# A graph attention layer and a mean-aggregation layer on one core: the neighbour lists cut into finer steps, the projected rows stored from another queue, and the second layer's products put in another order

## The chip, the core and the metric

The kernel runs on one core of a Trainium2 chip. A core has five engines that run side by side, each with its own instruction stream, executed in order: TensorE (PE in the profile, with PEld for the loading of its weights) for matrix products, VectorE (DVE), ScalarE (ACT), GpSimd (POOL) and SyncE (SP), which here only issues transfers. ACT and POOL can issue transfers too; each issuing engine has its own DMA queue, and 16 DMA engines serve all of them. On-chip data lies in SBUF, with 128 partitions; products are summed in PSUM. What is compared is the device time of one launch in microseconds (us).

## What is computed

Two layers over a graph of 4096 nodes with 512 features. `adj` is a 4096 x 4096 matrix of int32 zeros and ones, in which about one entry in a thousand is one, so a row has some four neighbours.

```python
# layer 0: attention with 8 heads of 64, then residual and layer norm
Wh = einsum('nf,hfo->hno', x, W)
f1 = einsum('hno,ho->hn', Wh, a[:, :64])
f2 = einsum('hno,ho->hn', Wh, a[:, 64:])
e = leaky_relu(f1[:, :, None] + f2[:, None, :], 0.2)
e = where(adj > 0, e, NEG_INF)
x = layernorm(x + einsum('hnm,hmo->hno', softmax(e), Wh))   # heads side by side

# layer 1: mean of the neighbours, two linear maps, a combining map, residual, layer norm
agg = mask @ x / maximum(deg, 1.0)
self_f, nb_f = x @ W_self + b_self, agg @ W_nb + b_nb
x = layernorm(x + relu(concat([self_f, nb_f]) @ W_comb + b_comb))
```

## The kernel before

The nodes are cut into 32 blocks of 128. Nothing of the 4096 x 4096 products is formed: the kernel turns each row of `adj` into a short list of neighbours, and then fetches the neighbours' rows with indirect transfers. All instructions stand in an order written out by hand; generators (`yield`) let a long piece of work be laid in portions between the blocks, one portion at each `next`; `some(lists)` takes one portion of each list in hand.

**First stage, the lists.** A loop over `b` does one block of `adj` per turn. SP loads `adj` in halves of 1 MB into four buffers, two blocks ahead (`load_adj`, L384), and blocks of `x` eight ahead (`load_x`, L317). ACT turns each half into bf16 masks (`mask_adj`, L393), which frees its buffer. PE folds the mask into keys in PSUM (`fold_adj`, L407), and DVE takes the largest (`max_keys`, L423). After every fourth block a `decode` (L430) turns the keys of four blocks into lists: bit operations (to L448), three passes of maxima per block (L454 to L456), counts and the first three neighbours (L459 to L469), ranks and placing matrices for the further ones (`lt` and `st`, L484 and L485), two shared slots (L494 to L518) and the owners of these slots (`own`, L520). It has six portions, and it is taken together with the one before it. `late_lists` (L529) then prepares for the first `NE` = 7 blocks which neighbours lie near the end of the graph. Beside it the nodes are projected: `transposed` (L325), two halves of products (`node_half`, L334), `node_rest` (L343), and `store` (L902), which writes the row of Wh and of f2 to the table `t0` in DRAM from ACT's queue, one turn later. A row has two buffers. Block 0 is projected ahead of the loop, so that block b + 1 falls in turn b, and from turn `AHEAD` = 10 block b + 2. The weights of layer 1 are multiplied together on the way: `m1` = W_self times the upper half of W_comb in this stage, `m2` = W_nb times the lower half between the stages (`fold_weights`, L267).

**The turn.** Behind the last `store` GpSimd gathers the rows of block 0 (L961) and so on: five indirect transfers per block, one per list slot, into `GA` = 5 buffers. Meanwhile the last lists and `m2` are worked on.

**Second stage, the attention.** The loop over `i` is a pipeline over blocks, in which weights (L626), exponentials, denominators (L636), weighted rows (L668), shared slots (`a_shared`, L680), layer norm, a transposition, and `z` = x times m2 (`a_z`, L716) follow each other. `z` goes to the table `t1`, the transposed x to `xt`. The rest of `m2`, the last `decode` and a sum of biases are laid between the turns i = -2 to 11.

**Third stage, the mean.** The first blocks are gathered from `t1` before its last rows are written: for blocks below NE, early gathers fetch what is there (`gather_early`, L604, 5 transfers a block), and one more per block brings the late rows when all of `t1` is written (`gather_late`, L607). For the others 5 full gathers a block go into `GB` = 7 buffers. Per block PE adds the product with m1 (`g_self`, L749, two blocks ahead), the shared slots (`g_shared`, L756) and for the first NE the late ones (`g_late`, L763); DVE sums the other slots (`g_adds`, L734) and forms the moments (`g_moments`, L772); ACT ends the norm (`g_norm`, L782), and SP stores the rows.

Of the kernel before, what the change touches and what calls it, by code (L numbers as in the profile page):

```python
# [56 lines left out]
NE = 7  # L57
# [33 lines left out]
def listed_layers(  # L91
# [33 lines left out]
    AHEAD = 10  # L125
# [141 lines left out]
    def fold_weights(loaded, m, place, tags):  # L267

        wr, wc = loaded

        def turned(c):
            tp = ps.tile([P, FB, P], F32, name="sm", bufs=2)
            for d in range(FB):
                nc.tensor.transpose(tp[:, d, :], wr[:, c, ts(d, P)], ident)
            wT = place(c)
            nc.scalar.copy(wT, tp.rearrange("p c r -> p (c r)"))
            return wT.rearrange("p (c r) -> p c r", c=FB)

        wT = turned(0)
        for c in range(FB):  # L280
            nxt = turned(c + 1) if c + 1 < FB else None
            yield
            tag = tags[c % 2]
            mp = ps.tile([P, HD], F32, name=tag, bufs=1 if tag in ("key", "tp") else 2)
            for d in range(FB):
                nc.tensor.matmul(
                    mp, lhsT=wT[:, d, :], rhs=wc[:, d, :], start=(d == 0), stop=(d == FB - 1)
                )
                if d % 2:
                    yield  # L290
            nc.scalar.copy(m[:, c, :], mp)
            wT = nxt
# [59 lines left out]
    def mean_row(w_sb, xacc, wp):  # L352
# [24 lines left out]
        nc.scalar.dma_start(t0[1:2, 0:H], mf)  # L377
        nc.scalar.dma_start(t0[1:2, H:TW], mr[0:1, 0:HD])
# [51 lines left out]
    def decode(b0, dp, place, slow=False):  # L430
# [4 lines left out]
        for k in range(2):  # L435
# [4 lines left out]
            nc.vector.tensor_sub(kk[:, :, k + 1, :], kk[:, :, k, :], top.bitcast(F32))  # L440
        kf = kk.rearrange("p g a c -> p (g a c)")
        ki = dp.tile([P, G * 3 * NC], I32, name="ki", bufs=1)
        nc.vector.tensor_copy(ki, kf)
        nc.vector.tensor_scalar(ki, ki, SC - 1, None, OP.bitwise_and)
        ke = dp.tile([P, G * 3 * NC], I32, name="ke", bufs=1)
# [7 lines left out]
        for g in range(G):  # L453
# [3 lines left out]
            if slow or g == G - 1:  # L457
                yield
# [11 lines left out]
        yield  # L470
# [4 lines left out]
        dg = dp.tile([P, G], F32, name="dg", bufs=1)  # L475
        nc.vector.tensor_scalar(dg, deg[:, bs], 1.0, None, OP.max)
        nc.vector.reciprocal(L[:, :, KL + 1], dg)

        sts = []
        for b in range(b0, b0 + G):  # L480
# [6 lines left out]
            if slow or b == b0 + G - 1:  # L487
                yield
        for g in range(G):
            if b0 + G < LB - G:  # L490
                nc.gpsimd.tensor_copy(of[:, b0 + g, :], sts[g])
            else:
                nc.scalar.copy(of[:, b0 + g, :], sts[g])
        pe = ps.tile([P, G, KH, EX + H], F32, name="sm", bufs=2)  # L494
        for g in range(G):
            for k in range(KH):
# [3 lines left out]
                )  # L500
        nc.vector.tensor_copy(es[:, bs], pe[:, :, :, 0:EX])
# [25 lines left out]
        )  # L527

# [67 lines left out]
    def gather(table, b, pool, at=None):  # L596
        g = pool.tile([P, KS, TW], F32, name="g")
# [273 lines left out]
    m1s = fold_weights(loaded, m1, lambda c: xs[:, NB - 12 + c, :], ("nm", "nm"))  # L871
    for k in range(3):
        next(m1s)
    bcol = bias_columns(brw)
    biased = fold_bias(loaded, bcol[:, 0:FB])
    for b in range(XL):
        sum_x(b, xacc)


    def node_block(w, xT, between=None):  # L880
# [6 lines left out]
        node_rest(w, row)  # L887
        return row
# [13 lines left out]
    def store(w, row):  # L902
        nc.scalar.dma_start(t0[2 + w * P : 2 + (w + 1) * P, :], row[:, 0:TW])

    row = node_block(0, xT)
    for k in range(3):
        next(m1s)
    xT = transposed(1, wp)
    for h in range(NH):
        mask_adj(0, h)  # L910
    key_bank(0)
    load_x(XL)
    sum_x(XL, xacc)
    w, lists = 1, []
    for b in range(LB):
        for k in range(1 + (b == AHEAD)):
            load_x(w + k + XL)
            sum_x(w + k + XL, xacc)
# [3 lines left out]
        some(lists)  # L922
# [61 lines left out]
    for k in range(3):  # L984
        some(lists)
# [529 lines left out]
```

## Time and profile before

| | us |
|---|---|
| three runs: median (lowest, highest) | 692.93 (691.37, 694.28) |
| the profiled execution, whole | 695.46 |
| its span, which all times below count from | 693.8 |
| PE busy, share of the span | 620.6, 89% |
| DVE busy | 495.9, 71% |
| ACT busy | 439.1, 63% |
| POOL busy | 383.4, 55% |

| stage, by the first and last instructions of its groups in the trace | from, to |
|---|---|
| halves of `adj` masked by ACT (L395) | 30.5 to 242.7 |
| first gather of the attention (L591) to last product of `a_z` (L719) | 238.5 to 493.0 |
| first `g_shared` of the mean (L758) to the end | 494.2 to 693.8 |

Engine rows count the time in which an instruction ran; a transfer that GpSimd issues counts there as busy for the time that its issue takes, and the data land some microseconds later. An engine can be busy for 89% on average and still be the limit in one stage and not in another, so the stages are read one by one.

### The profile page before, as it was taken

Reading aid. Unit: us, or ns where it says so; the run is one execution under the profiler, and the core shown is the slowest. Engines: PE = TensorE matmul, PEld = TensorE weight load, DVE = VectorE, ACT = ScalarE, POOL = GpSimd, SP = SyncE. Lnnn points to the kernel's source line nnn. Section 1 sums busy time; section 2 is a strip of 40 time slices with the busy share of each in tenths; the row PEclk is TensorE's granted clock in tenths of the full one; section 3 lists DMA queues with packets and bytes.
Section 4 is the critical chain, followed back from the end, with each engine's and each line's share of the span. In section 5 each row is a group of like instructions: output and inputs, shape, how many; then the busy total and the mean of one; then the engine's idle time right before and its main releaser. Section 6 shows DMA issues by size and latency. Waiting matters only on the chain.

```text
span 693.8 us, 8911 instructions
## 1 busy us (share of the span) xinstructions
PE 620.6 (89%) x2354; PEld 340.8 (49%) x2354; DVE 495.9 (71%) x1415; ACT 439.1 (63%) x922; POOL 383.4 (55%) x435
## 2 busy tenths in 40 slices
PE   5997989879899688999999999999869999999992
PEld 2565757547576444444545554555323444444430
DVE  6035877898896877999889899988322566565654
ACT  2377877775787634756677777766423566666754
POOL 6532222332211277766566677757776777777760
PEclk9999999999999889999999999999989999999996
DMA  8899999999999977888788999978988899999991
GB/s 269 327 382 320 399 406 407 407 407 385 322 404 375 347 232 230 273 262 255 214 260 277 273 280 281 272 253 263 307 241 266 282 306 317 311 305 304 305 305 72
DMA packets 94040, 209.89 MB, mean 303 GB/s; under 512 B 13649, under 2 KB 13657, under 8 KB 93982
## 3 DMA queue, kind: packets, MB, share of 16 engines
q1 hardware_dynamic: 61968, 111.95, 43.7%
q0 software_dynamic: 26160, 86.40, 42.0%
q10 hardware_dynamic: 5854, 10.90, 4.2%
q8 instruction: 21, 0.34, 0.2%
q14 instruction: 37, 0.30, 0.1%
HBM read 175.52 MB, written 33.69 MB: 302 GB/s over the span
## 4 chain that ended last, share of the span: by engine, by line
PE 50%; DVE 22%; DMA 9%; issue 6%; POOL 4%; ACT 4%; DVEq 0%; ACTq 0%; SPq 0%; POOLq 0%
PE pw L719 11%; PE pw L337 7%; PE nm L751 6%; PE nm L682 6%; PE pw L751 6%; POOL g L591 4%; PE pw L758 3%; PE nm L758 3%; DMA xT<-xt 2%; PE tp L329 2%; DMA g<-t,idx 2%; DVE row L341 2%; DMA t<-row 2%; PE sm L655 1%; DVE kk L428 1%
## 5 line engine op out<-in xcount | busy, mean ns | idle before, releaser
L591 POOL DMA_INDIRECT g<-t,idx x285 | 272.4, 956 | 109.6 <-issue 71.0
L337 PE MATMUL pw<-w_sb,xT 128*128 128x264 f32 x512 | 131.9, 403 | 15.8 <-DVE row L341 15.8
L395 ACT ACTIVATE ab<-at 128x2048 bf16<-128x2048 int32 x64 | 122.0, 1907 | 23.9 <-DMA at<-in_adj_dram 19.4
L719 PE MATMUL pw<-wr,xT 128*128 128x512 f32 x256 | 117.7, 602 | 0.7 <-ACT xT L331 0.7
L337 PEld LDWEIGHTS pw<-w_sb,xT 128*128 128x128 f32 x512 | 94.3, 194 | 44.9 <-DVE row L341 17.6
L323 POOL TENSOR_TENSOR xacc<-xacc,xs 128x512 f32<-128x512 f32 x32 | 41.3, 1291 | 81.3 <-DMA xs<-in_x_dram 80.9
L670 DVE TENSOR_TENSOR g<-g,key 128x1024 f32<-128x1024 f32 x64 | 77.9, 1216 | 1.1
L719 PEld LDWEIGHTS pw<-wr,xT 128*128 128x128 f32 x256 | 46.3, 190 | 47.3 <-issue 46.1
L682 PE MATMUL nm<-g,own 128*128 128x512 f32 x128 | 62.7, 612 | 0.0
L751 PE MATMUL nm<-m,xT 128*128 128x512 f32 x128 | 58.0, 596 | 4.5 <-DMA xT<-xt 4.5
L341 DVE COPY row<-pw 128x264 f32<-128x264 f32 x64 | 26.9, 422 | 47.9 <-PE pw L337 35.3
L751 PE MATMUL pw<-m,xT 128*128 128x512 f32 x128 | 57.8, 594 | 1.5 <-ACT nm L742 1.5
L348 POOL COPY f1s<-lst 128x24 f32<-128x24 f32 x32 | 11.7, 367 | 79.1 <-DVE lst L344 44.7
L331 ACT COPY xT<-tp 128x512 f32<-128x512 f32 x64 | 37.2, 582 | 26.2 <-PE tp L329 19.5
L705 ACT ACTIVATE xs<-y,ln_sum 128x512 f32<-128x512 f32 x32 | 23.1, 722 | 43.2 <-DVE y L698 43.2
L774 DVE SCALAR_TENSOR_TENSOR sm<-y,lst,nm 128x512 f32<-128x512 f32 x16 | 12.1, 755 | 49.8 <-PE nm L768 27.9
L329 PEld LDWEIGHTS tp<-ident,xs 128*128 128x128 f32 x256 | 30.0, 144 | 34.2 <-ACT xs L714 24.9
L329 PE MATMUL tp<-ident,xs 128*128 128x128 f32 x256 | 40.2, 280 | 7.1 <-ACT xs L714 5.8
L751 PEld LDWEIGHTS nm<-m,xT 128*128 128x128 f32 x128 | 24.1, 191 | 37.3 <-issue 32.1
L591 POOL DMA_INDIRECT g<-t,idxe x35 | 33.1, 947 | 15.4 <-issue 8.5
L751 PEld LDWEIGHTS pw<-m,xT 128*128 128x128 f32 x128 | 24.1, 190 | 32.2 <-issue 28.4
L742 ACT COPY nm<-brow 128x512 f32<-128x512 f32 x16 | 9.4, 590 | 44.3 <-DVE sm L774 44.3
(208 smaller groups left out, 1076.8 us busy)
## 6 DMA issues: line engine op xcount, KB each, us to landing
at<-in_adj_dram SPq DMA_DIRECT2D x64, 1024.0 KB, 9.2
t<-row ACTq DMA_DIRECT2D x32, 260.0 KB, 6.0
xt<-xT SPq DMA_DIRECT2D x32, 256.0 KB
t<-row SPq DMA_DIRECT2D x32, 256.0 KB, 3.9
xT<-xt SPq DMA_DIRECT2D x32, 256.0 KB, 7.9
out_dram<-row SPq DMA_DIRECT2D x32, 256.0 KB, 4.1
xs<-in_x_dram SPq DMA_DIRECT2D x31, 256.0 KB, 12.7
g<-t,idx POOLq DMA_INDIRECT x285, 4.6
```

What stands on the lines that cost most here:

```text
L323: nc.gpsimd.tensor_tensor(xacc, xacc, xs[:, b, :], OP.add)
L329: nc.tensor.transpose(tp[:, c, :], xs[:, b, ts(c, P)], ident)
L331: nc.scalar.copy(t, tp)
L337: nc.tensor.matmul(pw, lhsT=xT[:, c, :], rhs=w_sb[:, c, k * HW : (k + 1) * HW], start=(c == 0), stop=(c == FB - 1),)
L341: nc.vector.tensor_copy(row[:, k * HW : (k + 1) * HW], pw)
L395: nc.scalar.activation(ab, loads.pop((b, h)), AF.Relu, accum_out=asum[:, b, h : h + 1])
L591: nc.gpsimd.indirect_dma_start(out=out, out_offset=None, in_=table, in_offset=bass.IndirectOffsetOnAxis(ap=at, axis=0),)
L670: nc.vector.tensor_tensor(gv if to is None else to.rearrange("p (k h d) -> p k h d", k=1, h=H), gv, E[b][:, sl].unsqueeze(3).to_broadcast( ...
L682: nc.tensor.matmul(NM[b], lhsT=OWN[b][:, k, :], rhs=G0[b][:, K0 + k, H:TW], start=False, stop=(k == KH - 1), skip_group_check=True,)
L719: nc.tensor.matmul(pz, lhsT=xT[:, c, :], rhs=m2[:, c, :], start=(c == 0), stop=(c == FB - 1))
L751: nc.tensor.matmul(NM[b], lhsT=xT[:, c, :], rhs=m1[:, c, :], start=False, stop=(c == FB - 1), skip_group_check=True,)
L758: nc.tensor.matmul(NM[b], lhsT=OWN[b][:, k, :], rhs=g[:, K0 + k, 0:HD], start=False, stop=(k == KH - 1), skip_group_check=True,)
```

## The change

Six things are changed together.

1. The first stage starts with the lists: block 0 of `adj` is masked and its keys begun before the loop, block 0 is projected in turn 0 beside its own list, and two turns (14 and 19) project two blocks. `sum_x` runs four blocks behind the loads of x.
2. `m1` is folded in eight half columns, one in turn 0 and in every odd turn, instead of in full at the start; the second half is added by DVE.
3. `decode` has 16 portions, of which four are taken per turn (two before the block, two after), so that one is done when the next begins. Between the counts and the ranks three portions pass, and the copies of the placing matrices come behind the products that read them. `late_lists` starts two turns later, with `NE` = 6.
4. Wh rows are stored from GpSimd's queue right behind the block. The weights of `m2` are loaded by SP's queue.
5. Between the stages the decode of blocks 24 to 27 is finished, twelve of sixteen portions of `m2` are done, and half of the last decode; the rest goes into turns -2 to 6.
6. In the third stage `g_shared` and `g_late` of a block stand ahead of `g_self` of the block after next, and block 6 is gathered in full. A gather buffer is made once and filled slot by slot.

```diff
-NE = 7
+NE = 6
-    AHEAD = 10
+    AHEAD = (14, 19)
...
+    def turned(wr, c, wT):
+        tp = ps.tile([P, FB, P], F32, name="sm", bufs=2)
+        for d in range(FB):
+            nc.tensor.transpose(tp[:, d, :], wr[:, c, ts(d, P)], ident)
+        nc.scalar.copy(wT, tp.rearrange("p c r -> p (c r)"))
+        return wT.rearrange("p (c r) -> p c r", c=FB)
+    def fold_halves(loaded, m, place):
+        wr, wc = loaded
+        wT = turned(wr, 0, place(0))
+        yield
         for c in range(FB):
+            for k in range(2):
+                mp = ps.tile([P, HD], F32, name="nm", bufs=2)
+                for d in range(2 * k, 2 * k + 2):
+                    nc.tensor.matmul(
...
+                if k == 0:
+                    nc.scalar.copy(m[:, c, :], mp)
+                else:
+                    nc.vector.tensor_add(m[:, c, :], m[:, c, :], mp)
+                    if c + 1 < FB:
+                        wT = turned(wr, c + 1, place(c + 1))
+                yield
+    def fold_quarters(loaded, m, place):
+        wr, wc = loaded
+        wT = turned(wr, 0, place(0))
+        for c in range(FB):
+            nxt = turned(wr, c + 1, place(c + 1)) if c + 1 < FB else None
+            mp = ps.tile([P, HD], F32, name="tp", bufs=1)
             for d in range(FB):
                 nc.tensor.matmul(
                     mp, lhsT=wT[:, d, :], rhs=wc[:, d, :], start=(d == 0), stop=(d == FB - 1)
                 )
-                if d % 2:
-                    yield
-            nc.scalar.copy(m[:, c, :], mp)
+                if d == FB - 1:
+                    nc.scalar.copy(m[:, c, :], mp)
+                yield
             wT = nxt
...
+    def gather_buffer(k):
+        pool = ctx.enter_context(tc.tile_pool(name=f"gat{k}", bufs=1))
+        return pool.tile([P, KS, TW], F32, name="g")
+    def gather(table, b, g, at=None):
-        g = pool.tile([P, KS, TW], F32, name="g")
...
-    def store(w, row):
-        nc.scalar.dma_start(t0[2 + w * P : 2 + (w + 1) * P, :], row[:, 0:TW])
+    def store(w, row, eng=nc.scalar):
+        eng.dma_start(t0[2 + w * P : 2 + (w + 1) * P, :], row[:, 0:TW])
...
         node_rest(w, row)
+        store(w, row, nc.gpsimd)
...
+    w, lists = 0, []
+    for b in range(LB - 1):
+        for k in range(1 + (b in AHEAD)):
             load_x(w + k + XL)
+            sum_x(w + k + XL // 2, xacc)
         load_adj(b + 2, ap)
...
+        for k in range(2):
+            some(lists)
+        for k in range(1 + (b in AHEAD)):
+            nxt = transposed(w + 1, wp)
+            if k == 0:
+                key_bank(b + 1)
+                for h in range(NH):
+                    mask_adj(b + 1, h)
+            node_block(w, xT, None if k else b)
             w, xT = w + 1, nxt
+        for k in range(2):
+            some(lists)
+        if b == 0 or b % 2:
+            next(m1s, None)
...
+        if b == 16:
+            lates = late_lists(dp, fp.tile([P, FB * HD // P, P], F32, name="wr"))
...
         if b % G == G - 1:
-            lists = [*lists[-1:], decode(b + 1 - G, dp, on_own)]
+            lists = [decode(b + 1 - G, dp, on_own)]
...
     a_owners(0, wp)
     a_owned(0, wq)
-    lists = [decode(NB - G, dp, on_last, slow=True), *lists[-1:]]
-    for k in range(3):
+    for k in range(7):
         some(lists)
-    for k in range(4):
+    for k in range(12):
         next(m2s)
+    lists = [decode(NB - G, dp, on_last)]
+    for k in range(8):
+        some(lists)
...
+        if i == -2:
+            for k in range(2):
+                next(m2s)
...
-        for k in range({-2: 1, -1: 3, 0: 2}.get(i, 0)):
-            next(m2s, None)
-        if 2 <= i < 12:
+        for k in range({1: 4, 2: 2, 3: 1, 4: 1, 5: 1, 6: 1}.get(i, 0)):
             some(lists)
-        if 0 <= i < 4:
-            next(biased)
+        if i in (-1, 0):
+            for k in range(2):
+                next(biased)
...
     for b in range(NE):
         gather_late(b, gl)
+    for b in range(NE, GB):
+        G1[b] = gather(t1, b, gps[b])
...
     for b in range(NB):
         if b > 1:
             g_first(b, G1[b])
+            g_shared(b, G1[b])
+            if b < NE:
+                g_late(b, gl, wq)
         if b + 2 < NB:
             nxt = load_xT(b + 3, wp) if b + 3 < NB else None
             g_self(b + 2, xT, m1)
...
         if b > 1:
-            g_shared(b, G1[b])
-            if b < NE:
-                g_late(b, gl, wq)
             g_adds(b, G1[b], wq)
```

## The prediction

> **What bounds the kernel now.** I read first the transfers in windows of 5 us (columns: window, length, busy us and count of each engine, granted PE clock, mean busy share of the DMA engines, GB/s).
>
> ```profile
> 30.00:35.00 5.00, 3.55 (x25) 2.09 (x25) 0.43 (x1) 5.00 (x7) 4.77 (x6) 1.00 0.49 122
> ...
> 60.00:65.00 5.00, 4.16 (x26) 2.74 (x24) 3.37 (x11) 2.52 (x3) 1.61 (x2) 1.00 0.74 231
> ...
> 105.00:110.00 5.00, 4.69 (x24) 3.83 (x24) 2.31 (x10) 3.55 (x6) 2.84 (x4) 1.00 1.05 408
> ...
> 180.00:185.00 5.00, 3.90 (x26) 2.52 (x24) 4.73 (x21) 4.66 (x6) 2.42 (x2) 1.00 0.91 297
> ```
>
> The list stage is bound by transfers: at most 408 GB/s, with holes. Shortfalls below 407 GB/s between 10 and 235 us sum to 16 us of transfer: 3.5 at 30 to 35, 3.3 at 55 to 65, 4.5 at 165 to 190, 2.2 at 220 to 235, the rest small. No change can win more than these 16 there. DVE is busy 85% of 85 to 165, where transfers are full: it is the next bound.
>
> Then the timeline of the turn (start, length, engine, line, operation):
>
> ```profile
> 240.84 1.90 ACT L395 ACTIVATE ab<-at 128x2048 bf16<-128x2048 int32 x1
> ...
> 251.82 0.20 DVE L626 TENSOR_TENSOR e<-g,f1s 128x40 f32<-128x40 f32 x1 [0.30 <-issue]
> ...
> 252.58 0.67 PE L636 MATMUL sm<-e,own 128*128 128x8 f32 x4 [2.46 <-ACT e L630]
> ```
> ```profile
> 274.26 3.68 PE L719 MATMUL pw<-wr,xT 128*128 128x512 f32 x8
> ```
>
> The last mask (240.84) is two ACT masks behind the arrival of `adj`, which I put at 238. The first shared sum comes 14.6 us after, z(0) 36.3 after. z(10) stands at 350.82, hence 7.66 a block, against 6.66 from there on (z(30) at 484.38): the decode on DVE costs the first ten blocks 10 us. From z(10) PE is the bound.
>
> Last, the chain of waits and the timeline of the third stage:
>
> ```profile
> 506.60 5.40 DMA gl<-t,idxl
> 511.99 0.14 issue
> 512.13 2.04 PE nm L768 x2
> ```
> ```profile
> 673.74 0.95 POOL L591 DMA_INDIRECT g<-t,idx x1 [0.30 <-issue]
> ...
> 678.80 1.88 PE L758 MATMUL pw<-g,own 128*128 128x512 f32 x4
> ...
> 683.51 0.76 DVE L774 SCALAR_TENSOR_TENSOR sm<-y,lst,pw 128x512 f32<-128x512 f32 x1
> ```
>
> PE stands 5.5 us for the first late gather; then PE (3.43 + 1.72 = 5.15 us a block) and GpSimd (5 gathers of 0.95 + 0.30 = 6.25) both run nearly without a gap. GpSimd's head start of seven buffers is used up exactly at the end: its last gather goes out at 673.74, lands at the median 4.8 later (678.5), and the last shared product starts at 678.80. So both bound this stage.
>
> **What the skill says.** "DMA: Bandwidth & Descriptors", Queues, rings and completion order: each DMA engine takes turns between the queues it has work for. The trace agrees: x on SP's loaded queue lands after 12.7 us, a row on ACT's after 6.0. A store from GpSimd should thus also take some 6; no run here shows one. "SBUF — State Buffer", Who interferes with whom: VectorE and GpSimd share a port pair under an exclusive lock. The trace agrees: GpSimd's small copy takes 0.20, but 1.19 under DVE's `own` of 1.21 (L520). "TensorE: Matmul & The Clock Gate", What's actually happening: an idle PE falls to half clock and needs about 3.4 us of work to recover. Here the two late products take 2.04 after 5.5 us of idling and 1.02 later.
>
> **The change, part by part.** The sum is made against the profiled execution's 695.46 us (span 693.8 and 1.7 around it), 0.4% above the median.
>
> *List stage, -10.0.* (a) `adj` 0 is masked when it lands instead of at 30.48, behind node block 0 and the first fold of m1: the next `adj` load follows at some 22, while x still loads until 30. The hole at 30 goes: -3.5. (b) At 55 to 65 the chain shows DVE waiting 6.35 and 5.29 for a row's store that ACT issued a turn late. From GpSimd it goes out behind the small copy: 0.2 to 1.2 for the copy, about 1 for the issue (as a gather; up to 1.69 under the lock), 6 to land: some 9 against the 12.9 (two turns of 6.43, the transfer time of 2.62 MB) until the row is needed. Behind it on GpSimd stand `sum_x`, whose x now has come four turns earlier (70.7 us of waits for x vanish), and the `of` copies, with time to spare: POOL is a third busy. `pads` still takes a row here, so -2.0 of 3.3. (c) m1 in half columns takes 1.7 us a turn on PE instead of 3.4 and 0.6; four additions on DVE (0.7 each) hide. -1.0 of the 1.9 in 35 to 55 and 65 to 75. (d) One decode at four portions a turn: the heaviest turn has 1.7 (two placing pairs) + 1.9 + 1.2 + 2.05 (base: maxima 0.9, row copies 0.85, small 0.3) = 6.9 us of DVE, near the 6.43, where two decodes could meet before. But late lists (1.6 a turn from b = 16) meet a second node block (1.2) at 19: 9.7. I take -2.3 of 4.5. (e) At 220 to 235, PE's rank product no longer stands ahead of a mask's fold for an unready DVE (4.0 us, and ACT 4.0 behind it): -1.2 of 2.2. Bounds for the stage: -16 to -1.
>
> *Turn, +11.9 to the first shared sum.* PE's order now is: keys of block 31, decode's products, three columns of m2, shared sum 0. In the trace the maxima of 31 end at 245.59, 7.6 after `adj`. Then DVE 0.5 + four pairs at 0.98, and the last placing products: 12.5. m2: 3 x 3.43 + 4 x 0.6 = 12.7, plus 1.3 for half clock at its start: 26.5, against 14.6. DVE in parallel needs 3.9 + 0.5 + 1.9 + 1.2 + (decode, first half) 2.7 + 3.3 + 1.3 = 14.8, so 22.4: hidden by 4. Gathers start early enough to be hidden too. Bounds: m2 all at full clock (25) and all at half (36).
>
> *Shared sum 0 to z(0): 17.0 instead of 21.7, -4.7.* One column of m2 is left instead of three. Chain: sum and m2 2.8, weighting to `adds` 5.2, sums and biases (two of 0.7) 2.7, ACT's norm 3.1, transposition and copy 1.3, the next block's reach and wait 1.9.
>
> *z(0) to z(10): 71.2 instead of 76.6, -5.4.* Ten blocks at 6.66, plus what DVE cannot hide: 6.7 us of decode in turns 1 to 4, of which its idle 0.6 a block hides 2.1. Net of turn and attention: +11.9 - 4.7 - 5.4 = +1.8. Its bounds: -3 to +9.
>
> *Mean, -6.8.* GpSimd's early gathers shrink by 5 (6.26 us): late ones start at 500.35, after the last z landed (493.69 + 3.9). The first lands at 505.75; PE is done with its self products at 506.6 and goes on there instead of at 512.13. GpSimd then does 6 late and 5 more full ones, so block 7 starts 1.25 earlier; its wait of 2.81 before 530.32 (buffer of block 2) goes but for 0.3, since that block's shared product now stands ahead of a self product. Last gather at 670.0, landed 674.8, shared product to 676.7. Before, the shared products of 29 to 31 came 1.7 apart, and DVE and ACT ran 2.8 us behind (683.51); with gathers 6.25 apart they don't. Hence 683.51 becomes 676.7. PE alone would end at 506.6 + 168.5 - 0.9 - 2.0 = 672.2, so GpSimd is the bound. Bounds: -9 (landing 3.2) to -3 (the wait stays).
>
> The rest costs nothing: m2's weights on SP come behind the last `adj`, as before; slot by slot, a gather starts earlier, never later.
>
> Sum: -10.0 + 1.8 - 6.8 = -15.0; 695.46 to 680.5, ratio 0.978; of the median 692.93, **678**.
>
> **Rivals.**
> 1. *Forecast*, 678, own range 671 to 685: 0.50.
> 2. *Everything comes* (0.17): all 16 us of holes, turn neutral, -8: -24, hence 669. For it: ACT, PE and POOL have room. Against: DVE at 85%.
> 3. *The list stage stays DVE's* (0.17): DVE's in-order waits for PE (24.9 us for L337) keep the holes, -1 to -3 there; 695.46 - 2 + 1.8 - 6.8 = 688.5, of the median 686; half clock throughout m2 adds up to 7 and ends at no change.
> 4. *Slower: the store from GpSimd lands late* (0.10). Row buffers are needed again after 12.9 us. At a landing above some 10 us each further us costs half a us per block, 15 us in all, through DVE's row copy, PE, masks, `adj` loads. The list gain is gone at 10.7, and slower decides from about 11.2. At 12.5: -10 + 37 + 1.8 - 6.8 = +22, hence 715. For it: descriptors written under DVE's lock. Against: gathers land in 3.6 to 6.3 amid full transfers (238 to 255).
> 5. *No visible change* (0.06): 3 with half clock.
>
> **Numbers.** 678 is the likeliest. The range of 8 in 10 is 665 to 691: it leaves out case 4 and the edge of 2. About 0.5% (3.5 us) is what a measurement here can tell from no change. Faster: 0.50 + 0.17 + 0.15 of case 3 and a part of 5 = 0.83; same 0.07; slower 0.10.
>
> **What would show it.** Right: transfers at 400 GB/s through 30 to 65; last mask at some 230; shared sum 0 about 26 after `adj`; z in steps under 7.2 from z(0); first late product without idling PE before it; last gather some 4 us earlier relative to the last z; moments of block 31 right behind its shared product. Wrong: row copies waiting for stores, holes at 165 to 190 unchanged, PE at 0.85 per product through m2, or a third stage in which PE waits for gathers long before its end.

## The result: 702.3 us, 1.5% slower than before

| | before | after |
|---|---|---|
| median (lowest, highest), us | 692.15 (691.15, 694.28) | 702.31 (702.09, 704.77) |
| ratio of after to before, 95% interval | | 1.0151 (1.0116, 1.0185) |
| span of the profiled execution | 693.8 | 699.8 |
| DVE busy | 495.9 | 521.4 |

The medians lie 10.2 us apart, the spans of the two profiled executions 6.0: the one of the kernel before took 695.46 us, above all its timed runs here, and the one of the changed kernel 702.09, the lowest of its own. The marks of the prediction, read from both timelines, say where these 6.0 us come from; the other 4.2 can't be placed in a stage.

| step | from and to (before; after) | forecast | measured |
|---|---|---|---|
| list stage, to the start of the last mask | 240.84; 243.42 | -10.0 | +2.6 |
| last mask to first shared sum | to 252.58; 269.65 | +11.9 | +14.5 |
| first shared sum to z(0) | to 274.26; 288.88 | -4.7 | -2.4 |
| z(0) to z(10) | to 350.82; 364.60 | -5.4 | -0.8 |
| z(10) to the end of the span | to 693.8; 699.8 | -6.8 | -7.8 |
| sum | | -15.0 | +6.1 |

The experiments ran on several chips. On those of e1 to e4, e13, e14 and e18 the kernel before takes 693 to 696 us; on those of e5 to e12 and e15 to e17 it takes 781 to 787. There the stages behind the lists are longer (z(10) to the end 412 to 424 us in the changed kernels, instead of 335 to 338), so of these runs only the marks of the list stage are compared (where the kernel of e5 has 235.3 and 233.5 there, and 235.0 on an ordinary chip). A ratio is always to the kernel before on the same chip.

A mark comes from one traced execution, and it differs between executions of the same code. The start of the last mask is 240.8 in the kernel before and 244.9 in e1, which has the same list stage but for `NE`; with the changed list stage it is 243.4 (after), 243.2 (e2) and 245.9 (e7). A difference of 2 to 4 us at this mark thus says little: the list stage didn't become measurably slower, it lacks the forecast 10.

### The profile page after: what moved, and what is told of

Read it like the earlier page. It is cut to its first block, busy times and chain, and to the rows that moved or that the text cites. A ratio compares the mean times of both kernels' runs of the same rounds, so it can differ in the third digit from the quotient of the medians.

```text
span 699.8 us, 9126 instructions
## 1 busy us (share of the span) xinstructions
PE 624.7 (89%) x2350; PEld 345.6 (49%) x2350; DVE 521.4 (75%) x1416; ACT 440.5 (63%) x922; POOL 397.8 (57%) x468
## 5 line engine op out<-in xcount | busy, mean ns | idle before, releaser
L610 POOL DMA_INDIRECT g<-t,idx x290 | 277.5, 957 | 114.2 <-issue 54.6
L354 PE MATMUL pw<-w_sb,xT 128*128 128x264 f32 x512 | 135.5, 411 | 16.9 <-DVE row L358 16.9
L354 PEld LDWEIGHTS pw<-w_sb,xT 128*128 128x128 f32 x512 | 97.3, 200 | 47.5 <-DVE row L358 20.0
L365 POOL COPY f1s<-lst 128x24 f32<-128x24 f32 x32 | 8.4, 262 | 136.9 <-DVE lst L361 69.1
L704 PE MATMUL nm<-g,own 128*128 128x512 f32 x128 | 65.8, 638 | 0.0
L340 POOL TENSOR_TENSOR xacc<-xacc,xs 128x512 f32<-128x512 f32 x32 | 40.9, 1279 | 11.1 <-DMA xs<-in_x_dram 10.5
L773 PEld LDWEIGHTS nm<-m,xT 128*128 128x128 f32 x128 | 24.2, 190 | 32.4 <-issue 30.1
L610 POOL DMA_INDIRECT g<-t,idxe x30 | 28.5, 950 | 17.1 <-issue 6.4
L780 PE MATMUL pw<-g,own 128*128 128x512 f32 x64 | 31.5, 612 | 4.1 <-DMA g<-t,idx 3.1
```

What stands on the lines that cost most here:

```text
L340: nc.gpsimd.tensor_tensor(xacc, xacc, xs[:, b, :], OP.add)
L354: nc.tensor.matmul(pw, lhsT=xT[:, c, :], rhs=w_sb[:, c, k * HW : (k + 1) * HW], start=(c == 0), stop=(c == FB - 1),)
L610: nc.gpsimd.indirect_dma_start(out=out, out_offset=None, in_=table, in_offset=bass.IndirectOffsetOnAxis(ap=at, axis=0),)
L704: nc.tensor.matmul(NM[b], lhsT=OWN[b][:, k, :], rhs=G0[b][:, K0 + k, H:TW], start=False, stop=(k == KH - 1), skip_group_check=True,)
L773: nc.tensor.matmul(NM[b], lhsT=xT[:, c, :], rhs=m1[:, c, :], start=False, stop=(c == FB - 1), skip_group_check=True,)
L780: nc.tensor.matmul(NM[b], lhsT=OWN[b][:, k, :], rhs=g[:, K0 + k, 0:HD], start=False, stop=(k == KH - 1), skip_group_check=True,)
```

## The profile after

First the busy line of the page: engine, us, share of the span, instructions.

```profile
PE 624.7 (89%) x2350; PEld 345.6 (49%) x2350; DVE 521.4 (75%) x1416; ACT 440.5 (63%) x922; POOL 397.8 (57%) x468
```

DVE has one instruction more than before (1416 instead of 1415) and 25.5 us more to do. Four additions of m1 are new (2.7 us in all), and the late lists are a little shorter. Most of the rest is in instructions that stand in both kernels in equal number: L531 (a product of `decode`) takes 8.1 us more in its 8, L503 (`lt` of the placing matrices) 7.5 in its 32, L478 (slots marked) 5.6 in its 8.

Next the transfers in windows of 5 us, in the columns of the prediction (window, length, busy us of PE, PEld, DVE, ACT and POOL, granted PE clock, DMA share, GB/s).

```profile
30.00:35.00 5.00, 5.00 (x33) 3.44 (x32) 1.33 (x5) 3.07 (x4) 1.98 (x2) 1.00 1.05 410
60.00:65.00 5.00, 5.00 (x23) 3.67 (x24) 4.73 (x22) 3.56 (x4) 1.06 (x3) 1.00 1.05 406
105.00:110.00 5.00, 4.14 (x26) 2.73 (x24) 4.76 (x10) 3.75 (x5) 1.66 (x3) 1.00 1.05 410
165.00:170.00 5.00, 4.65 (x13) 3.70 (x14) 2.09 (x9) 0.00 (x0) 0.76 (x2) 0.66 0.80 304
170.00:175.00 5.00, 5.00 (x40) 4.20 (x38) 3.07 (x6) 1.59 (x3) 3.36 (x7) 1.00 0.14 55
180.00:185.00 5.00, 4.17 (x23) 3.00 (x24) 4.69 (x21) 3.60 (x5) 2.11 (x3) 1.00 0.86 315
```

The early holes (122 and 231 GB/s before) are filled, as forecast. At 158.84 SP issued the load of block 22, which it had issued at 167.67 before: a lead of 8.8 us. The load of block 23 went out at 176.44, before at 175.56: the lead was lost in one turn, in which ACT did no mask at all (0.00 from 165 to 170), so that no buffer came free.

The timeline of GpSimd and VectorE shows what stretches (start, length, engine, line, operation):

```profile
150.67 0.26 DVE L475 MAX8 nb<-kj 128x8 f32<-128x96 f32 x1
150.93 1.29 POOL L340 TENSOR_TENSOR xacc<-xacc,xs 128x512 f32<-128x512 f32 x1
150.96 1.32 DVE L478 TENSOR_SCALAR va<-nb 128x64 f32<-128x64 f32 x1
...
157.16 1.96 DVE L503 TENSOR_SCALAR lt<-iota,end 128x256 f32<-128x256 f32 x1
157.67 2.64 POOL L340 TENSOR_TENSOR xacc<-xacc,xs 128x512 f32<-128x512 f32 x2
159.22 1.37 DVE L504 SCALAR_TENSOR_TENSOR own<-iota,lst,lt 128x256 f32<-128x256 f32 x1
...
172.37 1.42 POOL L516 CAST of<-own 128x256 uint8<-128x256 f32 x4
172.59 0.29 DVE L519 COPY es<-sm 128x128 f32<-128x128 f32 x1 [1.00 <-PE sm L510]
172.80 0.22 DVE L520 COPY f1s<-sm 128x64 f32<-128x64 f32 x1
172.93 2.13 DVE L522 TENSOR_TENSOR kx<-pidx,es 128x8 f32<-128x8 f32 x1
173.77 1.26 POOL L340 TENSOR_TENSOR xacc<-xacc,xs 128x512 f32<-128x512 f32 x1
...
244.41 0.20 DVE L478 TENSOR_SCALAR va<-nb 128x64 f32<-128x64 f32 x1
...
247.78 0.36 DVE L503 TENSOR_SCALAR lt<-iota,end 128x256 f32<-128x256 f32 x1
```

The marking of the slots that hold a neighbour (L478) takes 0.20 us where GpSimd is idle (244.41); beside an addition of x (L340) it starts 0.03 after it and ends 0.06 after it. The addition of 128 x 512 and the instruction of 128 x 64 don't run side by side. A small difference of 128 x 8 (L522) takes 2.13 instead of 0.16, through a cast and the addition behind it. But the copies of L519 and L520, which read PSUM, run at their usual length under the casts.

The turn and the end, in the same form:

```profile
243.42 1.89 ACT L412 ACTIVATE ab<-at 128x2048 bf16<-128x2048 int32 x1
...
246.47 1.04 POOL L610 DMA_INDIRECT g<-t,idx  x1 [6.48 <-issue]
...
252.99 1.95 PE L270 MATMUL sm<-ident,wr 128*128 128x128 f32 x8
254.76 5.33 PE L303 MATMUL tp<-wc,row 128*128 128x512 f32 x8
...
260.76 3.70 PE L303 MATMUL tp<-wc,row 128*128 128x512 f32 x8 [0.24 <-ACT wr L307]
...
264.03 0.20 DVE L648 TENSOR_TENSOR e<-g,f1s 128x40 f32<-128x40 f32 x1 [0.41 <-issue]
...
269.65 0.61 PE L658 MATMUL sm<-e,own 128*128 128x8 f32 x4 [0.81 <-ACT e L652]
...
276.34 1.96 PE L704 MATMUL nm<-g,own 128*128 128x512 f32 x4
...
284.70 3.76 PE L704 MATMUL nm<-g,own 128*128 128x512 f32 x4
```
```profile
519.48 0.95 POOL L610 DMA_INDIRECT gl<-t,idxl  x1 [0.30 <-issue]
520.14 1.02 PE L790 MATMUL nm<-gl,ol 128*128 128x512 f32 x2
...
683.88 0.95 POOL L610 DMA_INDIRECT g<-t,idx  x1 [0.30 <-issue]
...
690.00 0.76 DVE L796 SCALAR_TENSOR_TENSOR sm<-y,lst,pw 128x512 f32<-128x512 f32 x1 [3.03 <-PE pw L780]
```

Three columns of m2 stand ahead of the first shared sum, as the order says, and the first eight products take 5.33 us instead of 3.70, at a granted clock of 0.50 from 245 to 258. From about 282 the clock is 0.50 again, until past 288, and the four products of L704 take 3.76 us instead of 1.96. At the end the late products take 1.02 (2.04 before) and have no idle PE ahead of them; from the last z to the last gather it is 180.8 us (683.88 - 503.13), before 184.4 (673.74 - 489.34).

## The experiments

To compare the stretch, each VectorE group of the list stage (12 to 230 us) is taken at its median where no addition or cast of GpSimd overlaps it; what overlapped instructions take above that median is summed. **S** is that sum, **M** the start of the last mask. S is time by which instructions are longer, not time lost by the stage: what a longer instruction costs there depends on what waits for it.

| kernel | S under additions + under casts | M |
|---|---|---|
| before | 8.6 + 1.2 | 240.8 |
| e1 (list stage as before, but for `NE`) | 11.6 + 1.9 | 244.9 |
| after | 21.0 + 9.1 | 243.4 |
| e2 (list stage as after) | 18.7 + 11.2 | 243.2 |
| e7 (list stage as after) | 18.7 + 11.2 | 245.9 |
| e3 | 18.3 + 0.1 | 241.0 |
| e6 | 10.9 + 5.2 | 240.5 |
| e5, e9, e13 (one kernel) | 3.4 + 3.0, 3.2 + 2.7, 3.2 + 2.2 | 235.3, 233.5, 235.0 |
| e4 | 0 + 1.7 | 227.2 |
| e10, e14 (one kernel) | 0.6 + 0, 0.6 + 0 | 228.1, 226.0 |

In after the worst groups under additions are L503 (7.9) and L478 (5.5), under casts a product of L531 (8.3). The maxima of L473, which read SBUF, were under additions 9 times and gained less than 0.1 us in all.

**The third stage alone on the kernel before (e1).**

```diff
-NE = 7
+NE = 6
+    for b in range(NE, GB):
+        G1[b] = gather(t1, b, gps[b])
...
             g_first(b, G1[b])
+            g_shared(b, G1[b])
+            if b < NE:
+                g_late(b, gl, wq)
```

> The kernel before with the third stage's part of the change alone (six late blocks, block 6 gathered in full, shared products ahead of self products, gather buffers slot by slot). Theory: this part is what it was forecast to be, and what came between z(10) and the end in the changed kernel (-7.8): about 685, ratio 0.989, and the late product follows the self products with no idle PE. Rival: part of the -7.8 belongs to the other parts (z and gathers stand otherwise to each other after a later turn): 689 or more.

687.13 us, ratio 0.987 (0.981 to 0.993), near the 685 of the theory and below the rival's 689. From z(10) to the end 335.7, before 343.0: -7.3. The part does alone what it does in the whole.

```profile
505.80 3.70 PE L754 MATMUL nm<-m,xT 128*128 128x512 f32 x8 [3.22 <-DMA xT<-xt]
509.34 3.60 PE L754 MATMUL pw<-m,xT 128*128 128x512 f32 x8
512.77 1.02 PE L771 MATMUL nm<-gl,ol 128*128 128x512 f32 x2
```

The timeline of e1 shows the late product right behind the self products, where PE stood for 5.5 us before.

**The jam of turn 19 (e3).**

```diff
-    AHEAD = (14, 19)
+    AHEAD = (10, 14)
```

> The changed kernel with the second extra projected block at turn 14 instead of 19 and the first at 10, so that none meets the late lists. Theory A: the jam of turn 19 (extra block, late lists, last decode portions, two additions) loses the 8 to 10 us of lead that transfers had: last mask at some 234, in all 692 to 695. Rival B: VectorE is stretched everywhere by GpSimd's additions and casts, and the lead is lost elsewhere: last mask after 240, 700 or more.

702.29 us, ratio 1.010 (1.008 to 1.013); M 241.0. The hole of 55 GB/s is gone (262 over 170 to 180, where after has 104), but smaller holes stand elsewhere (330 over 150 to 160, 282 over 180 to 190). Theory A's forecast (234, 692 to 695) is missed, rival B's is met. Turn 19 explains 2.4 us at most, which is within the spread of the mark: it is only where the loss showed first. (S falls by 11.7 here, and M by those 2.4.)

**No additions of x (e4).**

```diff
-            sum_x(w + k + XL // 2, xacc)
```

> The changed kernel without the additions of x on GpSimd from turn 0 on (the mean row, which only rows without neighbours read, holds less than it should). Theory B: these additions stretch VectorE's operations beside them; without them VectorE's busy time falls by some 15 us of the 25 that it rose, the holes after 160 fill, last mask at 234 to 237: 693 to 697. Rival A: the jam of turn 19 stays as it is: last mask after 240, 700 or more.

686.66 us, ratio 0.988 (0.982 to 0.994), 15.6 below e3 on the same chip; M 227.2; DVE busy 497.3 instead of 521.4. Turn 19 begins with the masks of block 20 here too, at 151.98 and 155.23; the windows of e4 from there:

```profile
155.00:160.00 5.00, 4.25 (x23) 3.73 (x23) 2.88 (x11) 2.48 (x3) 0.74 (x2) 1.00 1.05 404
160.00:165.00 5.00, 5.00 (x36) 3.91 (x36) 3.79 (x13) 2.88 (x4) 2.16 (x6) 1.00 1.05 411
165.00:170.00 5.00, 4.69 (x29) 3.85 (x27) 4.69 (x19) 3.73 (x7) 0.56 (x2) 1.00 1.01 366
```

The turn has its extra block, its late lists and its decode as in after, and yet transfers stay full, and the next mask starts at 163.12, 7.9 us after the second of block 20; in after it was 15.7 (158.72 to 174.41). So theory B holds, and it came out larger than it was expected (693 to 697, last mask at 234 to 237). It doesn't yet say how the additions harm: by VectorE's stretch, or by standing ahead of the stores on GpSimd.

**The additions kept, but at another moment (e5, e9, e13).**

```diff
         node_half(w, 0, xT, w_sb, row)
+        if w + XL // 2 < NB:
+            tk = small.tile([P, 1], F32, name="tk", bufs=1)
+            nc.gpsimd.tensor_copy(tk, row[:, 0:1])
+            sum_x(w + XL // 2, xacc)
...
-            sum_x(w + k + XL // 2, xacc)
```

> The changed kernel, whole computation, with each addition of x held back on GpSimd behind a one-column copy of the row's first half, so that it runs while VectorE takes maxima and copies from PSUM. Theory B (the additions cost because VectorE's SBUF operations stand still under them): stretch under additions falls from 21 us to under 3, last mask at some 229, 687 to 690, ratio to before 0.99. Rival F (the additions cost because rows' stores and small copies queue behind them on GpSimd): they still stand ahead of the store, so nothing is won: 700 or more.

> The same kernel as e5_placed, for its time: that run's chip took 781 us for the kernel before, with slow gathers after the list stage. Theory B: 687 to 691 where the kernel before takes 692, ratio 0.993 to 0.999, last mask at 230 to 236. Rival F: ratio 1.01 or more, last mask after 240.

> The kernel of e9_placed_again, for its time on a chip where the kernel before takes its 692 to 695 us: with the last mask 8 to 10 us earlier than in the changed kernel (233 to 236 in both runs so far against 243 and 246) and everything behind it as in the changed kernel, theory B gives 690 to 695, ratio 0.995 to 1.002. Rival F: 700 or more, ratio over 1.01.

On the ordinary chip (e13) 693.42 us, ratio 1.004 (1.000 to 1.008), against 1.015 for the changed kernel; M 235.0; time and mark are as theory B forecast for this run. On the other chips M was 235.3 and 233.5 (the first forecast, 229, was too low), with times of 793.07 and 795.67, ratios 1.010 and 1.021. In the timeline of e13 the addition waits for the first half of the row, and VectorE works on PSUM meanwhile:

```profile
98.81 0.42 DVE L358 COPY row<-pw 128x264 f32<-128x264 f32 x1
99.16 0.88 DVE L445 MAX8 kk<-nm 128x8 f32<-128x128 f32 x4
99.38 0.18 POOL L909 COPY tk<-row 128x1 f32<-128x1 f32 x1 [3.59 <-DVE row L358]
99.52 1.26 POOL L340 TENSOR_TENSOR xacc<-xacc,xs 128x512 f32<-128x512 f32 x1
100.82 0.17 DVE L361 COPY lst<-row 128x8 f32<-128x8 f32 x1
```

Four maxima from PSUM take 0.88 under the addition, as without it. The additions are all there and still ahead of the store, so rival F falls for what is won here: it is the moment that costs. M improves by 8 to 10 us, half to three fifths of what leaving the additions out gives. That the rest isn't F's either is seen in e14 below: M reaches 226.0 with all additions ahead of the store.

**The additions eight blocks ahead, as before (e6).**

```diff
-    for b in range(XL // 2):
+    for b in range(XL):
...
-            sum_x(w + k + XL // 2, xacc)
+            sum_x(w + k + XL, xacc)
```

> The changed kernel with the additions of x eight blocks ahead, as before, so that each waits for its x. Theory B: the additions run at the landing of x, at other moments of the turn, and collide less, but the row's store stands behind an addition that waits for x and comes late; the two about cancel: 696 to 704, and rows wait for their buffers (over 15 us in all). Rival F: no different from any other place ahead of the store: 700 to 704 without waits for row buffers.

799.33 us on a slower chip; M 240.5. S under additions is 10.9, half of after's: the wait for x (38.6 us in all) moves them. Rows wait 13.5 us for their stores, against 4.2 in after. Both halves of theory B's expectation are seen, the second a little weaker than forecast (over 15).

**The last row alone from ScalarE (e7), and all rows (e12).** e7 stores block 31 from ACT behind its mask; e12 is e9 with

```diff
-        store(w, row, nc.gpsimd)
...
             nxt = transposed(w + 1, wp)
+            if w > 0:
+                store(w - 1, row)
...
```

> The changed kernel with the last row alone stored from ScalarE behind the mask, as before. Theory: on GpSimd the first gather stands 6.1 us behind that store, on ScalarE 3.1 us; but in the changed turn m2's products hide the gathers, so the first shared sum comes no earlier: 700 to 703, first gather about 3 us earlier. Rival: the turn hangs on the first gather: 698 to 699.

> e9_placed_again with the rows stored from ScalarE a turn late, as before, instead of from GpSimd. Theory: the stores from GpSimd are worth the forecast 2 us in the list stage and cost 3 before the first gather: within 3 us of e9_placed_again. Rival C (the stores on GpSimd are themselves harmful, by their descriptors under VectorE's lock): 5 us or more faster than e9_placed_again.

e7 (804.30 us on a slower chip): the store goes out at 240.55 and the first gather at 247.75, 7.2 us later; in the changed kernel, from GpSimd, it was 7.0 (239.44 to 246.47): a miss for the theory that GpSimd's own store is slow to land. e12: M 231.5 against 233.5 and 235.3 of the same kernel with stores from GpSimd, 797.63 us against 795.67. That is within 3 us, as the theory said, and 2 us of M are within the spread. The queue of the stores makes no difference that these runs can tell: neither the 2 us of gain that the prediction gave it, nor the harm of rival C.

**The turn of the kernel before (e2).** m2 with `fold_weights` in the portions of before, and the last decode one portion a block.

> The changed kernel with the turn of the kernel before: m2 in portions through the first blocks of attention, the last decode one portion a block; list stage and third stage as changed. Theory: the turn's new order costs the +14.5 - 2.4 - 0.8 = +11.3 that the trace shows: about 691, ratio to the changed kernel 0.984, the first shared sum some 15 us after the last mask. Rival: the turn is late because the lists of the last blocks end later (full adj, slow clock), whatever the order: 699 or more.

702.74 us, ratio 1.011 (1.004 to 1.017). The first shared sum comes 18.7 us after the last mask (26.2 in after, 11.7 before), z(0) 40.4 (45.5 and 33.4). Undoing the order gives back 7.5 at the sum and 5.1 at z(0), but nothing of the time that these runs can tell: the median is 702.74, that of the changed kernel 702.31, of e3 on the same chip 702.29. The theory (691) is missed, the rival's 699 or more is met.

**Put together (e8, e10, e14).** e8 has the additions held back, extra blocks at 10 and 14, before's turn, and the last row stored from ACT. e10 adds three edits, of which two take the last collisions away:

```diff
+        if k == 1:
+            nc.vector.tensor_copy(lst[:, b, KL + 3 :], pw[:, TW - HW : FW - HW])
...
-            if b0 + 2 * G < LB:
+            if b0 < 0:
...
-    loaded = load_fold(1, w_nb, fp, nc.sync)
+    loaded = load_fold(1, w_nb, fp, nc.scalar)
```

> Additions held back as in the first of these runs, extra blocks at turns 10 and 14, the turn of the kernel before, the last row stored from ScalarE; list stage and third stage otherwise as changed. If the parts add up: last mask at some 228 (-14 to before), the turn as before (+-2), third stage -7.5: 692 - 14 - 7.5 = 671, ratio to before 0.969. Rival: the turn's gathers and lists are late whatever is done, +5: 676 or more.

> e8_combo (additions held back, extra blocks at 10 and 14, turn of the kernel before, last row stored from ScalarE), with the small f1 columns copied from PSUM instead of from the row, the casts of the placing matrices on ScalarE, and m2's weights loaded from ScalarE behind the last row's store as before. Theory: stretch of VectorE under GpSimd below 2 us, the first gather some 3 us behind the store of the last row instead of 6 to 7, since the 2 MB of weights no longer go ahead of it: 672 to 678, ratio 0.975. Rival: the 6 us are GpSimd's own and not the weights': the first gather still 6 us behind, 677 to 682.

> The kernel of e10_combo, for its time on such a chip: last mask at 228 (-12.8 to before), turn as before within 2 us, third stage -7.5: 672 to 676, ratio 0.97 to 0.976. Rival: the turn stays 7 us longer than before, as it did in e2_bturn: 679 to 682.

```profile
219.98 0.36 ACTq L961 DMA_DIRECT2D t<-row  x1
...
225.98 1.89 ACT L440 ACTIVATE ab<-at 128x2048 bf16<-128x2048 int32 x1
226.02 1.06 POOL L638 DMA_INDIRECT g<-t,idx  x1 [6.15 <-DMA t<-row]
```

e14 (timeline above): **682.15 us, ratio 0.981 (0.975 to 0.987)**, faster than both kernels. M is 226.0, 14.9 before the kernel before. Of the 9.0 us from e13 to e14, the extra blocks at 10 and 14, the copies and the casts weren't told apart. The forecast 672 to 676 is missed, the rival's 679 to 682 is met: z(0) comes 42.0 after the last mask. On the slower chips e8 took 787.65 (M 232.7, forecast 228) and e10 779.38 (M 228.1); e10, the kernel of e14, gains nothing there (ratio 0.998, 0.994 to 1.003), so the 2% are shown for one ordinary chip. GpSimd still waits 6.15 us for the first gather of e14, so m2's weights ahead of it on SP's queue were not what delays it. From e8 to e10, S falls from 8.5 to 0.6 and M by 4.6 us.

**What holds the turn (e11, e15 to e18).** e11 and e16 take a third extra block at turn 18, so that the last row is stored a turn earlier; e15, e17 and e18 are one kernel, e14 with more decode ahead of the last maxima and the last decode behind the first weights.

```diff
+        if b == LB - 2:
+            for k in range(4):
+                some(lists)
...
+    for k in range(3):
+        some(lists)
...
     for k in range(7):
-        some(lists)
-    lists = [decode(NB - G, dp, on_last)]
-    for k in range(6):
-        some(lists)
-    for k in range(4):
         next(m2s)
+    lists = [*lists, decode(NB - G, dp, on_last)]
...
```

> e10_combo with a third extra block at turn 18, so that the last row is stored in the last turn of the loop, from GpSimd. Theory: the first gather leaves GpSimd before the last mask (some 6 us before), the first shared sum no longer waits for gathers: 670 to 676, ratio 0.97. Rival: the third extra block costs a full turn's slack in the list stage (5 us of ScalarE and TensorE) and gives back what it wins: 675 to 680.

> e14_combo_time with eight instead of four decode portions in the last turn of the loop, the placing pairs of blocks 24 to 27 ahead of the last maxima, and the whole last decode behind the first block's weights (two portions a block at first, then one), m2 right behind the placing products. Theory (the turn is late because VectorE does 9 us of decode between the last maxima and the first weights, and TensorE's m2 waits behind it at half clock): first shared sum some 13 us after the last mask instead of 18.6, z(0) 36 to 38 after it instead of 42, and half of that lost again at the decode in the first blocks: 676 to 680, ratio 0.972 to 0.978. Rival: the first weights wait for the first gather and not for VectorE: sum and z(0) within 2 us of e14_combo_time, 681 to 685.

> e15_early with a third extra block at turn 18, so that the last row is stored a turn earlier and the first gather no longer stands behind it. Theory: the first gather leaves before the last mask and the first weights wait for nothing, 2 to 4 us below e15_early. Rival: the third extra block takes the list stage as much as it gives the turn, within 2 us of e15_early or above it.

> The kernel of e15_early, on a chip where the kernel before takes its 692 to 695 us (on the slower one the first weights waited for the gather: last mask 230.7, first shared sum 260.1). Theory (VectorE's decode ahead of the first weights makes the turn late): first shared sum some 13 us after the last mask, z(0) 36 to 38, 676 to 680. Rival (the first gather makes it late): sum and z(0) within 2 us of e14_combo_time (18.6 and 42.0 after the last mask), 681 to 685.

> The kernel of e15_early once more, for a chip where gathers are not slow. Theory (VectorE's decode ahead of the first weights makes the turn late; in e14_combo_time the gathers landed after 3.5 to 6.2 us, and the decode ran without a gap from 237.95 to the first weights at 243.86): first shared sum some 13 us after the last mask, z(0) 36 to 38, 676 to 680. Rival (the first gather makes it late): within 2 us of e14_combo_time there, 681 to 685.

e11, e15, e16 and e17 (782.25, 786.48, 785.50, 783.08 us) ran on the slower chips, with ratios of 0.995 to 0.999, and tell little of the turn; e11's first gather does leave at 225.4, ahead of its last mask at 227.1. e18: 687.27 us, ratio 0.989 (0.985 to 0.992), a miss for the theory and for the rival. (The trace is of an execution of 691.3 us, 4 above the median.) The last mask slips to 231.8: ScalarE stands for 5.8 us before a mask at 227.5. Ahead of that mask in its order is the store of the last row, which goes out at 225.93; VectorE copies this row out of PSUM only at 225.07 to 225.9, behind 5.7 us of decode without a gap. Timeline of e18:

```profile
225.93 0.35 ACTq L961 DMA_DIRECT2D t<-row  x1
...
229.02 1.06 POOL L638 DMA_INDIRECT g<-t,idx  x1 [3.20 <-DMA t<-row]
...
238.28 1.95 PE L318 MATMUL sm<-ident,wr 128*128 128x128 f32 x8
240.09 5.23 PE L330 MATMUL pw<-wc,row 128*128 128x512 f32 x8
241.14 0.19 DVE L676 TENSOR_TENSOR e<-g,f1s 128x40 f32<-128x40 f32 x1
245.16 0.60 PE L318 MATMUL sm<-ident,wr 128*128 128x128 f32 x4
245.60 3.60 PE L330 MATMUL pw<-wc,row 128*128 128x512 f32 x8
249.04 0.60 PE L318 MATMUL sm<-ident,wr 128*128 128x128 f32 x4
250.50 0.61 PE L686 MATMUL sm<-e,own 128*128 128x8 f32 x4 [0.86 <-ACT e L680]
```

The first weights (L676) come 9.3 us after the last mask, in e14 17.9: VectorE's decode did hold them there, and not the gather. But the sum now stands behind m2 on PE, 18.7 after the mask as in e14 (18.6). Two chains of nearly one length lie side by side, and taking one away shows the other.

## Why the prediction was wrong, by its own steps

Forecast and measured span lie 21.1 us apart (-15.0 and +6.1). The list stage makes 12.6 of it, the turn 2.6, first sum to z(0) 2.3, z(0) to z(10) 4.6; the mean gives 1.0 back.

**List stage, -10.0: the step that failed.** The parts that fill the holes were right where nothing else came in between: 30 to 65 us run at full rate, and with the collisions gone (e14) the last mask comes 14.9 us earlier, within the forecast's bounds of -16 to -1. What failed is the sentence in part (b): "Behind it on GpSimd stand `sum_x`, whose x now has come four turns earlier (70.7 us of waits for x vanish), and the `of` copies, with time to spare: POOL is a third busy." GpSimd had room for the wait, as the prediction says, but the wait decided when an addition ran. Without it each ran at the head of a turn, where VectorE does the SBUF work of the decode, and S rose from 9.8 to 30.1 us. Part (d) then summed VectorE's load (6.9 us in the heaviest turn, 9.7 in turn 19) from durations of the kernel before, as if they were properties of the instructions. e4, e5 and e13 show the cause: with the additions left out or moved, the same kernel reaches its last mask 16.2 and 8 to 10 us earlier. What made up the rest in e14 is shown in part: the copies and casts that still collided are worth some 4.6 us (e8 to e10), little more than the spread of the mark.

The passage that the prediction cited, the Trainium skill's "SBUF — State Buffer", Who interferes with whom, states the rule in full: a VectorE instruction with two SBUF inputs, or in a two-port mode, and a GpSimd instruction that reads SBUF block each other for the whole instruction, while one with at most one SBUF input outside these modes doesn't contend. The trace agrees on both sides: L522 and L531, with two SBUF inputs, are stretched, and the maxima, with one, gain less than 0.1 in nine overlaps. L478, with one, is stretched too (0.20 becomes 1.32); that it runs in a two-port mode is not shown by any run. The prediction applied it to the issue of the stores and to one small copy of GpSimd, and not to VectorE's decode, which was moved beneath the additions. Rival 3 (the list stage stays VectorE's) had the right engine, with a gain of 1 to 3 where no gain came (M 2.6 later, within its spread).

**Store from GpSimd (rival 4).** The stores land after 5.5 us in the median; the slower side came from another mechanism.

**Turn, +11.9: right in kind, 2.6 short.** Last mask to last placing products is 9.7 us in both the prediction's working and the trace. m2 was put at 12.7 + 1.3; from 253.16, when the last of these products ends, to the sum at 269.65 it is 16.5. The half clock isn't what is missing: it made eight products take 5.33 instead of 3.70, and 1.6 is about the 1.3 that was put for it, although the clock came back only some 6 us after PE's steady work began at 252.12, later than the 3.4 us that the prediction took as its rule. The three columns were put at 3.43 each and take 3.70 without it (0.8 in all), the transpositions and waits between them take 3.0 instead of 2.4, and at the end PE waits 0.8 for ScalarE's exponentials, which stand behind its copy of the third column. The bounds held the sum. (The working put the arrival of `adj` at 238; the last packets on SP's queue move at about 236. Only differences enter the sum.)

**First shared sum to z(0), -4.7, measured -2.4**, and **z(0) to z(10), -5.4, measured -0.8.** The first left out that PE idles once m2 no longer fills its waits (it is busy 0.75 us between 278 and 282, and the clock then falls to 0.50): the four shared products ahead of z(0) take 3.76 us at half clock, 1.8 of the missing 2.3. The second rested on VectorE hiding 2.1 of 6.7 us of decode in its idle time. It has none there: the first five blocks take 41.4 us, 8.1 more than five at 6.66 (6.68 by the prediction's own marks). All orders looked at on ordinary chips leave 75.7 to 77.0 us for these ten blocks (before, after, e1 to e4, e13, e14, e18), so where the last decode goes is nearly indifferent.

**Mean, -6.8: right.** -7.8 in the changed kernel, -7.3 alone on the kernel before; GpSimd's lead, the late products and the last moments moved as the steps say (the last gather 3.6 us earlier after the last z, forecast some 4).

**What stays open:** why the turn with before's order of m2 is still 7 to 9 us longer from the last mask to z(0) (40.4 and 42.0 against 33.4). In the kernel before the placing products of blocks 24 to 27 start at 239.54, ahead of the last mask, and in the changed one they end at 253.16, behind the last keys; e18 moved this work and gained nothing in sum (43.1 to z(0)). The rest of the stretch under casts that e3 lost by another placing of its extra blocks wasn't followed up either.

## What to carry to other kernels

A wait on an engine that has time to spare can be what keeps its work out of the way of another engine: before taking such a wait away, ask beside what the work will run then, and whether the two share ports. When an engine's busy time rises at an equal count of instructions, compare the lengths of single instructions with and without the neighbour's work, since means of groups hide it. And shared-port work can stay on GpSimd if a dependency pins it to a stretch in which VectorE reads PSUM: here the same additions cost 21 us of VectorE's time, or 3 (e13).

## What the runs showed of the hardware

- A GpSimd addition of 1.29 us holds up a VectorE instruction of 0.20 until it is done, and two GpSimd instructions in a row can do it through both: 2.13 us for one of 0.16, under a cast and an addition. Some 30 additions in the list stage thus made VectorE's instructions 21 us longer.
- Under additions, maxima, copies out of PSUM and a sum with one operand in PSUM kept their lengths (the last seen once in a trace). A copy of 128 x 8 within SBUF didn't: it lost 3.6 us in 15 overlaps in e13, and once it read PSUM (e14), S under additions was 0.6.
- The first gather waits until the last stored row has landed. GpSimd stood 3.1 to 3.5 us before it in the kernel before, e1, e15, e17 and e18, and 5.9 to 7.7 in all others. The queue doesn't decide it (the row is stored from ScalarE in e7, e10, e12 and e14 too), nor do m2's weights, which go out right behind the store in e14 as in e18. What does go with it is how much of `adj` is still under way. In the five with the short wait the store goes out 6.3 us or more behind SP's last load of `adj`, in the others 5.7 or less. In e14 `adj` still moves until about 224, and the row, stored at 219.98, lands at 225.15, 5.2 us later; in e18 it is done at about 224.2, and the row, stored at 225.93, lands 2.2 later. No run changes this alone.
